# A graph layer with a softmax over sorted edges: its scans one after the other in place of side by side, and a first batch of 24 groups

## The chip, the cores and the metric

The kernel runs on one core of a Trainium2 chip. A core has five engines that run their own instruction streams and wait for one another through semaphores: TensorE (PE in the profile), VectorE (DVE), ScalarE (ACT), GpSimd (POOL) and SyncE (SP). Here SyncE and ScalarE also start plain transfers, and GpSimd starts the indirect ones, the gathers. The metric is the device time of one execution in microseconds (us).

## The reference

The program is one attention layer of a graph network and a layer norm. There are 12,500 nodes with 64 features, and 400,000 edges with 64 features, sorted by destination; all is float32.

```python
h_src, h_dst = x[src], x[dst]
e = leaky_relu(concat([h_src, h_dst, efeats]) @ W_attn + b_attn, 0.01)[:, 0]
m = concat([h_src, efeats]) @ W_ne
emax = segment_max(e, dst, N)
ex = exp(e - emax[dst])
alpha = ex / segment_sum(ex, dst, N)[dst]
z = segment_sum(alpha[:, None] * m, dst, N)
out = relu(concat([x, z]) @ W_out)
return layernorm(x + out)
```

## The kernel before

**Groups, parts, batches.** 512 edges form a group: 128 partitions with 4 edges each. There are 782 groups. Four groups are a part, which has a tile of edge features (`ze`) and a tile of gathered source rows (`zx`). Up to 32 groups are a batch, the unit of the softmax. Before, `sizes` is one batch of 4, then 37 of 20, then one each of 20, 10 and 8: 41 batches. Both tiles have ten buffers (`ZB`), two batches of five parts.

**The start.** While the node features come in, VectorE computes for each node its share of the score as a source and as a destination (L429, L432). The source score goes as a 65th column into a copy of the features in memory (`table`); the destination scores (`sdflat`) are copied out as a row of 48 neighbours for each node (`shifted`). Seven gathers take from it, for each group, the 48 scores that its destinations can have (`wk`, L469), and ScalarE's queue writes them to `wins`. Gathers that are issued ahead of these seven cannot take rows of `table`; they take rows of x (`plain`), and such a batch computes its source scores itself in `scores` (L194, L196). Before, the first batch of one part is plain. Each gather brings one row to each of 128 partitions, so a part is 16 gathers (L167).

**A batch.** `scores` computes, part by part, the score of each edge: the product with the edge weights and its sum (L190, L192), the source score (L197), a one-hot matrix of the edge's destination among 48 slots (L199), which picks the destination's score (L204, L207), and the leaky relu (L209). `softmax` then works on the whole batch. The scores are transposed (L295) so that a row holds 128 edges in order, and a segment's maximum and sum are formed by scans along rows. As a segment can cross rows, each scan is done in three steps: every row by itself, then one scan on a single partition over the ends of the rows, then every row again from its right start. `to_rows` brings the ends of the rows to one partition (a transpose L215 and four copies L218), `to_cols` brings the starts back (four copies L224 and a transpose L227). Before, forward and backward scans go through this together, as two blocks of one tile, once for the maximum and once for the sum. The sums give `alpha` (L347), and `fac`, by which the column that the batch shares with the one before is scaled (L374). `aggregate` weights the one-hot matrices with alpha (L358) and multiplies them with `ze` and `zx` on TensorE (L366); VectorE adds the result into `acc` at the group's first destination (L376). Masks for the next batch are prepared in the same stretch (L256 to L276). Finished blocks of nodes are written back in between (L498 to L529, "write-back" in what follows).

**Order.** A scheduler puts the instructions of each engine in order; VectorE then executes them in that order. A gather into a tile waits for the last matmul of the batch that had it, by a dependency written out in `gather`, so that all tiles of a batch come free together. GpSimd's queue holds the gathers in order and nothing else of note. The indices for the gathers come through TensorE transposes and a cast on VectorE (`srcs`, L134), in three buffers, so that a cast also waits for the gathers that still read the buffer.

Of the kernel before, what the change touches and what calls it, by code (L numbers as in the profile page):

```python
# [9 lines left out]
F32 = mybir.dt.float32  # L10
I32 = mybir.dt.int32
AF = mybir.ActivationFunctionType
OP = mybir.AluOpType
AX = mybir.AxisListType

P = 128
# [7 lines left out]
FLOOR = -1e31  # L24

S = 48
BG = 32
SG = 4
BS = 20
HQ = 4  # L30
# [10 lines left out]
def sorted_path(ctx, tc, x, dst, idx, edge, w_ne, w_attn, b_attn, w_out, out, flag):  # L41
# [6 lines left out]
    nc = tc.nc  # L48
# [11 lines left out]
    const = ctx.enter_context(tc.tile_pool(name="const", bufs=1))  # L60
# [5 lines left out]
    ones_row = const.tile([1, P], F32, name="ones_row")  # L66
    nc.vector.memset(ones_row, 1.0)

    turn = const.tile([P, 3, BG], F32, name="turn")
    nc.vector.memset(turn, 0.0)  # L70
    turn4 = const.tile([P, 4, BG], F32, name="turn4")
    nc.vector.memset(turn4, 0.0)
    b_col = const.tile([P, 1], F32, name="b_col")
    wne = const.tile([P, D], F32, name="wne")
    wout = const.tile([D, 2, D], F32, name="wout")
# [21 lines left out]
    tiny = loop.enter_context(tc.tile_pool(name="tiny", bufs=2))  # L97
# [111 lines left out]
        nc.vector.scalar_tensor_tensor(yb, sdst[:, 0:n], SLOPE, sdst[:, 0:n], op0=OP.mult, op1=OP.max)  # L209
        return hot  # L210

    def to_rows(pair):

        tr = rows.tile([P, 2, BG], F32, name="tr")
        nc.vector.transpose(tr, pair[:, :, 0:BG])  # L215
        row = tiny.tile([1, 2, P], F32, name="row", bufs=1)
        for h in range(HQ):
            nc.vector.tensor_copy(row.rearrange("o k (g h) -> o h k g", h=HQ)[:, h], tr[h * BG:h * BG + 1])  # L218
        return row

    def to_cols(row, n):

        for h in range(HQ):
            nc.vector.tensor_copy(turn[h * BG:h * BG + 1, 0:n, :],  # L224
                                  row[:, 0:n, 0:P].rearrange("o k (g h) -> o h k g", h=HQ)[:, h])
        ct = rows.tile([P, 3, BG], F32, name="ct", bufs=2)
        nc.vector.transpose(ct[:, 0:n, :].rearrange("r k g -> r (k g)"), turn[:, 0:n, :].rearrange("r k g -> r (k g)"))  # L227
        return ct

    def neighbours(g0, G):  # L230

# [19 lines left out]
    def softmax(G, y, d3, carry, first):  # L251


        R = HQ * G
        far = rows.tile([P, P + 2], F32, name="far3")
        nc.vector.tensor_scalar(far, d3, FAR, None, op0=OP.mult)  # L256

        pf = rows.tile([P, P], F32, name="pf")
        nc.vector.tensor_tensor(pf, far[:, 0:P], far[:, 1:P + 1], op=OP.subtract)
        pb = rows.tile([P, P], F32, name="pb")  # L260
        nc.vector.tensor_tensor(pb, far[:, 1:P + 1], far[:, 2:P + 2], op=OP.subtract)
        same = rows.tile([P, P], F32, name="same")
# [1 line left out]
        up = tiny.tile([P, 1], F32, name="up")  # L264
        nc.vector.tensor_reduce(up, pf, axis=AX.X, op=OP.max)
        nc.vector.tensor_tensor(worst[:, 1:2], worst[:, 1:2], up, op=OP.max)
        same_b = rows.tile([P, P], F32, name="same_b")
        nc.vector.tensor_scalar(same_b, pb, 0.0, None, op0=OP.is_ge)

        nc.vector.tensor_tensor(turn4[:, 0:2, 0], far[:, 0:2], far[:, P:P + 2], op=OP.subtract)  # L270
        nc.vector.tensor_scalar(turn4[:, 2:4, 0], turn4[:, 0:2, 0], 0.0, None, op0=OP.is_ge)
        tr4 = rows.tile([P, 4, BG], F32, name="tr4")
        nc.vector.transpose(tr4.rearrange("r k g -> r (k g)"), turn4.rearrange("r k g -> r (k g)"))
        rw = tiny.tile([1, 4, P], F32, name="rw", bufs=1)
        for h in range(HQ):
            nc.vector.tensor_copy(rw.rearrange("o k (g h) -> o h k g", h=HQ)[:, h], tr4[h * BG:h * BG + 1])  # L276

        mrow = tiny.tile([1, 2, P + 2], F32, name="mrow")
        srow = tiny.tile([1, 3, P + 2], F32, name="srow")
        ROW1 = P + 1  # L280
        flat_m = mrow.rearrange("o k i -> o (k i)")
        flat_s = srow.rearrange("o k i -> o (k i)")
        top, rtm = flat_m[:, 0:P + 1], flat_m[:, ROW1:ROW1 + P + 1]
        den, rts = flat_s[:, 0:P + 1], flat_s[:, ROW1:ROW1 + P + 1]
        nc.vector.memset(rtm[:, R:P + 1], FLOOR)
        nc.vector.memset(rts[:, R:P + 1], 0.0)
        if first:
            nc.vector.memset(top[:, 0:1], FLOOR)
            nc.vector.memset(den[:, 0:1], 0.0)
            nc.vector.memset(srow[:, 2, 0:P], 1.0)  # L290
        else:
            nc.vector.tensor_copy(top[:, 0:1], carry[0])

        er = rows.tile([P, T, P // T], F32, name="er")
        nc.vector.transpose(er.rearrange("r t q -> r (t q)"), y.rearrange("p t g -> p (t g)"))  # L295
        e = rows.tile([P, P], F32, name="e")
        nc.scalar.activation(e.rearrange("r (q t) -> r q t", t=T), er.rearrange("r t q -> r q t"), AF.Copy)
        pair = rows.tile([P, 2, P], F32, name="pair")
        nc.vector.tensor_tensor_scan(pair[:, 0, ::-1], pf, e, FLOOR, OP.add, OP.max)
        nc.vector.tensor_tensor_scan(pair[:, 1, ::-1], pb[:, ::-1], e[:, ::-1], FLOOR, OP.add, OP.max)  # L300
        row = to_rows(pair)
        nc.vector.tensor_tensor_scan(top[:, 1:P + 1], rw[:, 0, :], row[:, 0, :], top[:, 0:1], OP.add, OP.max)
        nc.vector.tensor_tensor_scan(rtm[:, 0:R][:, ::-1], rw[:, 1, 0:R][:, ::-1], row[:, 1, 0:R][:, ::-1],
                                     FLOOR, OP.add, OP.max)
        ini = to_cols(mrow, 2)
        s2 = rows.tile([P, P], F32, name="s2")
        nc.vector.tensor_tensor_scan(s2, pf, e, ini[:, 0, 0:1], OP.add, OP.max)
        b2 = rows.tile([P, P], F32, name="b2")
        nc.vector.tensor_tensor_scan(b2[:, ::-1], pb[:, ::-1], e[:, ::-1], ini[:, 1, 0:1], OP.add, OP.max)
        dl = rows.tile([P, P], F32, name="dl")  # L310
        nc.vector.tensor_tensor(dl, s2, b2, op=OP.max)
        nc.vector.tensor_tensor(dl, e, dl, op=OP.subtract)
        ex = rows.tile([P, P], F32, name="ex")
        nc.scalar.activation(ex, dl, AF.Exp)
        if not first:

            drop = tiny.tile([1, 2], F32, name="drop")
            nc.vector.tensor_tensor(drop[:, 0:1], top[:, 0:1], rtm[:, 0:1], op=OP.max)
            nc.vector.tensor_tensor(drop[:, 1:2], top[:, 0:1], drop[:, 0:1], op=OP.subtract)
            nc.scalar.activation(drop[:, 1:2], drop[:, 1:2], AF.Exp)  # L320
            nc.vector.tensor_tensor(den[:, 0:1], carry[1], drop[:, 1:2], op=OP.mult)
        pair = rows.tile([P, 2, P], F32, name="pair")
        nc.vector.tensor_tensor_scan(pair[:, 0, ::-1], same, ex, 0.0, OP.mult, OP.add)
        nc.vector.tensor_tensor_scan(pair[:, 1, ::-1], same_b[:, ::-1], ex[:, ::-1], 0.0, OP.mult, OP.add)
        row = to_rows(pair)
        nc.vector.tensor_tensor_scan(rts[:, 0:R][:, ::-1], rw[:, 3, 0:R][:, ::-1], row[:, 1, 0:R][:, ::-1],
                                     0.0, OP.mult, OP.add)
        nc.vector.tensor_tensor_scan(den[:, 1:P + 1], rw[:, 2, :], row[:, 0, :], den[:, 0:1], OP.mult, OP.add)
        if not first:

            fac1 = tiny.tile([1, 2], F32, name="fac1")
            nc.vector.tensor_tensor(fac1[:, 0:1], rts[:, 0:1], den[:, 0:1], op=OP.add)
            nc.vector.reciprocal(fac1[:, 1:2], fac1[:, 0:1])
            nc.vector.tensor_scalar(srow[:, 2, 0:P], den[:, 0:1].to_broadcast([1, P]), fac1[:, 1:2], None, op0=OP.mult)
        ini = to_cols(srow, 3)
        nc.vector.tensor_tensor_scan(s2, same, ex, ini[:, 0, 0:1], OP.mult, OP.add)
        sm = rows.tile([P, P], F32, name="b2")
        nc.vector.tensor_tensor_scan(sm[:, ::-1], same_b[:, ::-1], ex[:, ::-1], ini[:, 1, 0:1], OP.mult, OP.add)

        nc.vector.tensor_tensor(s2, s2, ex, op=OP.subtract)  # L340
        nc.vector.tensor_tensor(sm, sm, s2, op=OP.add)
        nc.vector.reciprocal(sm, sm)
        al = rows.tile([P, T, P // T], F32, name="al")
        nc.vector.tensor_tensor(al.rearrange("r t q -> r q t"), ex.rearrange("r (q t) -> r q t", t=T),
# [3 lines left out]
        nc.scalar.activation(alpha, alpha0, AF.Copy)  # L348
        fac = None
        if not first:  # L350
            fac = tiny.tile([P, 1], F32, name="fac")
            nc.vector.tensor_copy(fac, ini[:, 2, 0:1])
        return fac, (top[:, R:R + 1], den[:, R:R + 1])

    def aggregate(g0, n, ze, zx, hot, b0, fac):
# [24 lines left out]
    sizes = []  # L380
# [4 lines left out]
    while left > 0:  # L385
        sizes.insert(0, min(left, BS))
        left -= sizes[0]
    starts = [sum(sizes[:k]) for k in range(len(sizes))]


# [22 lines left out]
    ahead = [gather(0, min(SG, sizes[0]), prepared[0][0], 0, True)]  # L413
# [6 lines left out]
    with before:  # L420

        before.enter_context(tc.issue_after(casts[0]))
        for c0 in range(0, NB, CB):
            c1 = min(c0 + CB, NB)
            n = c1 - c0
# [10 lines left out]
            if c0 == 3 * CB:  # L436
                d0f = pre.tile([1, NG], F32, name="d0f", bufs=1)
                nc.vector.tensor_copy(d0f, d0i)
                for g0 in range(0, NG, 3 * P):
                    n = min(3 * P, NG - g0)  # L440
                    pb = psum.tile([P, SG, P], F32, name="pg", bufs=4).rearrange("p k n -> p (k n)")
# [8 lines left out]
        zero = pre.tile([1, S], F32, name="zero", bufs=1)  # L450
        nc.vector.memset(zero, 0.0)
        nc.scalar.dma_start(out=sdflat[NB * P:NB * P + S].unsqueeze(0), in_=zero)
        while len(ahead) < 5 and (len(ahead) + 1) * SG <= sizes[0]:
            ahead.append(gather(len(ahead) * SG, SG, prepared[0][0], 0, True))
        NW = (NG + P - 1) // P
        d0p = pre.tile([P, NW], I32, name="d0p", bufs=1)
# [9 lines left out]
        for k in range(NW):  # L466
            m = min(P, NG - k * P)
# [6 lines left out]
    rows = loop.enter_context(tc.tile_pool(name="rows", bufs=1))  # L474
# [62 lines left out]
    k = 0  # L537
# [12 lines left out]
    with loop:  # L550
        carry = added = None
        done = []
        ready = {0: prepare(0), 1: prepare(1, listed(starts[1], sizes[1]))}
        for k, G in enumerate(sizes):
# [9 lines left out]
            for g0 in range(b0, b0 + G, SG):  # L564
                n = min(SG, b0 + G - g0)
# [4 lines left out]
            fac, carry = softmax(G, y, d3, carry, k == 0)  # L570
# [464 lines left out]
```

## Time and profile before

| | |
|---|---|
| time, median of 3 runs (lowest to highest) | 5173.82 us (5171.24 to 5175.08) |
| the profiled execution | 5171.24 us, span 5169.4 us |
| busy: POOL, DVE, PE, ACT | 2967.6 (57%), 2102.8 (41%), 654.6 (13%), 245.5 (5%) us |
| gathers (L167) from `table` and from x | 3112 and 16 |
| one gather, median interval between starts | 0.95 us, 1.25 us |
| moved by transfers | 249.24 MB, mean 48 GB/s |
| chain of work that ended last | issue 52%, DVE 26%, unknown queue 11%, PE 7% |

The profile comes from one execution. A row of a group gives the line of the kernel, the engine and the operation, the tiles that it writes and reads, how often it ran, the time that the engine was busy with it, the mean length of one in ns, and how long the engine had been idle just before, with what ended most of that. "issue" is time in which the engine waited for nothing that the profile shows, and "remote" a release by something that the profile does not know. In a timeline the first two numbers are the start, in us from the start of the span, and the length; the bracket has the idle time ahead of it. No engine is busy for much more than half of the span.

### The profile page before, as it was taken

The page shows a single profiled execution, that of the slowest core. Times are in us where ns is not written, and L with a number is a line of the kernel's source. Part 1 is how long each engine was busy: PE and PEld are TensorE (multiplying, and loading weights), DVE is VectorE, ACT ScalarE, POOL GpSimd, SP SyncE. Part 2 cuts the span into 40 slices and gives each one's busy share as a digit, 9 for nine tenths or more (in the row PEclk, how much of TensorE's full clock was granted, in tenths as well). Part 3 has the DMA queues.
Part 4 walks back from the last instruction along what each step waited for, and adds up shares of the span by engine and source line. Part 5 has one row for each costly group of instructions (what it writes and reads, how often), then busy time and mean ns, then how long its engine had stood idle before and what let it go on. Part 6 is the DMA issues. An engine that isn't in the chain of part 4 may idle for free.

```text
span 5169.4 us, 39994 instructions
## 1 busy us (share of the span) xinstructions
PE 654.6 (13%) x13346; PEld 608.8 (12%) x13346; DVE 2102.8 (41%) x5756; ACT 245.5 (5%) x527; POOL 2967.6 (57%) x3142
## 2 busy tenths in 40 slices
PE   0010000001111110111110110111111111111113
PEld 0010000001101010111110110110111111111113
DVE  4153343333343343443444344444344444444446
ACT  0000000000000000000000000000000000000001
POOL 4745665665556556556565655555555555555550
PEclk9985555555555555555555555555555555555555
DMA  7122222222222222222222222222222222222220
GB/s 134 28 50 47 47 47 47 47 47 46 49 46 47 46 49 47 49 47 49 47 49 47 49 48 47 48 48 47 49 48 48 48 48 48 48 47 47 47 44 11
DMA packets 304916, 249.24 MB, mean 48 GB/s; under 512 B 125446, under 2 KB 253870, under 8 KB 304699
## 3 DMA queue, kind: packets, MB, share of 16 engines
q0 software_dynamic: 100320, 104.46, 13.5%
q1 hardware_dynamic: 177690, 135.46, 9.6%
q10 hardware_dynamic: 26688, 6.67, 0.7%
q8 instruction: 107, 1.75, 0.1%
q14 instruction: 111, 0.90, 0.1%
HBM read 239.69 MB, written 9.07 MB: 48 GB/s over the span
## 4 chain that ended last, share of the span: by engine, by line
issue 52%; DVE 26%; another core or an unknown queue 11%; PE 7%; DMA 2%; SPq 1%; DVEq 1%; POOL 0%; ACT 0%; ACTq 0%
PE pg L366 5%; DVE prod L190 3%; DVE hot L199 2%; DVE y L192 2%; DVE acc L376 2%; DVE prod L204 1%; DVE sdst L207 1%; PE pg L513 1%; DVE turn L224 1%; DVE row L218 1%; DVE rw L276 1%; PE pg L512 1%; DVE tr L215 1%; DMA zx<-table,srcs 1%
## 5 line engine op out<-in xcount | busy, mean ns | idle before, releaser
L167 POOL DMA_INDIRECT zx<-table,srcs x3112 | 2942.0, 945 | 2007.7 <-PE pg L366 1018.8
L366 PE MATMUL pg<-w,ze 128*64 128x48 f32 x6256 | 470.2, 248 | 3531.4 <-DVE w L358 2031.3
L366 PEld LDWEIGHTS pg<-w,ze 128*64 128x64 f32 x6256 | 462.4, 165 | 3536.7 <-DVE w L358 1940.2
L366 PE MATMUL pg<-w,zx 128*64 128x48 f32 x6256 | 471.3, 248 | 30.4 <-issue 30.3
L366 PEld LDWEIGHTS pg<-w,zx 128*64 128x64 f32 x6256 | 462.0, 165 | 32.6 <-issue 32.6
L218 DVE COPY row<-tr 1x64 f32<-1x64 f32 x328 | 77.0, 235 | 554.4 <-issue 459.6
L192 DVE TENSOR_REDUCE y<-prod 128x16 f32<-128x1024 f32 x196 | 237.6, 1212 | 4.8 <-remote 4.8
L190 DVE TENSOR_TENSOR prod<-ze,fixed 128x1024 f32<-128x1024 f32 x196 | 237.3, 1211 | 0.0
L376 DVE TENSOR_TENSOR acc<-acc,pg 128x48 f32 x782 | 154.3, 197 | 140.5 <-remote 85.5
L207 DVE TENSOR_REDUCE sdst<-prod 128x16 f32<-128x768 f32 x196 | 186.1, 949 | 27.1 <-issue 11.2
L204 DVE TENSOR_TENSOR prod<-hot,win 128x768 f32<-128x768 bf16 x196 | 186.4, 951 | 2.5 <-DVE y L197 2.0
L199 DVE TENSOR_TENSOR hot<-fixed,drel 128x768 bf16<-128x768 f32 x196 | 185.8, 948 | 0.0
L358 DVE TENSOR_TENSOR w<-hot,fixed 128x768 f32<-128x768 bf16 x196 | 175.9, 947 | 18.9 <-ACT fixed L348 18.8
L134 DVE CAST srcs<-pp 128x80 int32<-128x80 f32 (+3 forms) x41 | 9.4, 230 | 336.1 <-DMA zx<-table,srcs 333.3
L224 DVE COPY turn<-mrow 1x64 f32<-1x64 f32 x164 | 37.0, 226 | 266.7 <-issue 245.4
L131 PE MATMUL pp<-ident,nat 20*128 20x20 f32 (+3 forms) x328 | 42.7, 270 | 737.4 <-issue 402.1
L131 PEld LDWEIGHTS pp<-ident,nat 20*128 20x128 f32 (+3 forms) x328 | 39.2, 198 | 745.2 <-issue 722.5
L186 ACT ACTIVATE win<-wrow 128x192 f32<-128x192 f32 x196 | 64.9, 331 | 1147.8 <-DVE prod L204 768.1
L276 DVE COPY rw<-tr 1x128 f32<-1x128 f32 x164 | 45.8, 279 | 178.5 <-issue 160.7
L215 DVE STREAM_TRANSPOSE tr<-pair 128x64 f32<-128x64 f32 x82 | 20.1, 245 | 213.1 <-remote 189.9
L348 ACT ACTIVATE fixed<-alpha 128x128 f32<-128x128 f32 x41 | 11.5, 281 | 1929.6 <-DVE alpha L347 1895.2
L224 DVE COPY turn<-srow 1x96 f32<-1x96 f32 x164 | 50.9, 310 | 124.4 <-issue 122.3
(131 smaller groups left out, 1228.6 us busy)
## 6 DMA issues: line engine op xcount, KB each, us to landing
ze<-in_edge_dram SPq DMA_DIRECT2D x194, 512.0 KB
zx<-table,srcs POOLq DMA_INDIRECT x3112
wrow<-wins SPq DMA_DIRECT2D x195, 96.0 KB
table<-xt ACTq DMA_DIRECT2D x14, 227.5 KB
xb<-in_x_dram ACTq DMA_DIRECT2D x24, 128.0 KB
out_dram<-yo SPq DMA_DIRECT2D x24, 128.0 KB
raw<-in_idx_dram SPq DMA_DIRECT2D x38, 80.0 KB
xt<-in_x_dram SPq DMA_DIRECT2D x13, 224.0 KB
```

The costliest lines, as they stand in the source:

```text
L167: got = nc.gpsimd.indirect_dma_start(out=zx[:, g, t, 0:D] if plain else zx[:, g, t, :], out_offset=None, in_=x[:, :] if plain else table[: ...
L190: nc.vector.tensor_tensor(prod[:, 0:n], ze[:, 0:n], w_edge.unsqueeze(1).to_broadcast([P, n, T, D]), op=OP.mult)
L192: nc.vector.tensor_reduce(yb, prod[:, 0:n], axis=AX.X, op=OP.add)
L199: nc.vector.tensor_tensor(hot[:, 0:n], slots.unsqueeze(1).unsqueeze(1).to_broadcast([P, n, T, S]), drel[:, :, b:b + n].rearrange("p t g -> ...
L204: nc.vector.tensor_tensor(at[:, 0:n], hot[:, 0:n], win[:, 0:n].unsqueeze(2).to_broadcast([P, n, T, S]), op=OP.mult)
L207: nc.vector.tensor_reduce(sdst[:, 0:n], at[:, 0:n], axis=AX.X, op=OP.add)
L218: nc.vector.tensor_copy(row.rearrange("o k (g h) -> o h k g", h=HQ)[:, h], tr[h * BG:h * BG + 1])
L224: nc.vector.tensor_copy(turn[h * BG:h * BG + 1, 0:n, :], row[:, 0:n, 0:P].rearrange("o k (g h) -> o h k g", h=HQ)[:, h])
L276: nc.vector.tensor_copy(rw.rearrange("o k (g h) -> o h k g", h=HQ)[:, h], tr4[h * BG:h * BG + 1])
L358: nc.vector.tensor_tensor(w[:, 0:n], hot[:, 0:n], alpha[:, :, b:b + n].rearrange("p t g -> p g t").unsqueeze(3).to_broadcast([P, n, T, S]) ...
L366: last = nc.tensor.matmul(pg[at:at + D, g, :], z[:, g, t, 0:D], w[:, g, t, :], start=(t == 0), stop=(t == T - 1))
L376: added = nc.vector.tensor_tensor(ag, ag, pg[:, g, :], op=OP.add)
```

## The change

The change has two parts.

`softmax` no longer runs its two directions side by side. The forward scan of the maximum is completed first (a scan, `to_row`, a scan on one partition, `to_col`, a scan); the backward scans then run over its result, so that they give the maximum of the whole segment. The sum goes the same way. So there are four round trips of a row of 32 values per partition group where there were two of a pair of rows. The mask of the backward direction for the sum (`same_b`) goes, as do the maximum of the two directions and the subtraction and addition that joined the two sums. `fac` is no longer carried through `to_cols`, but is brought to all partitions by four copies and a transpose of its own. In the program after, these lines are: `to_row` L215 and L218, `to_col` L228 and L223, the row scans L283, L293, L298, L306, L314 and L327, the scans on one partition L290, L302 and L325, alpha L334, fac L339 to L344, the weights L350, the matmuls L358, the scaling and the additions L366 and L368.

The first two batches are joined into one of 24 groups, six parts, which leaves 40 batches. All six parts are gathered from x, ahead of the seven gathers of the destination scores.

```diff
-    def to_rows(pair):
-        tr = rows.tile([P, 2, BG], F32, name="tr")
-        nc.vector.transpose(tr, pair[:, :, 0:BG])
...
+    def to_row(block):
+        tr = rows.tile([P, BG], F32, name="tr")
+        nc.vector.transpose(tr, block)
+        row = tiny.tile([1, P], F32, name="row", bufs=1)
+        for h in range(HQ):
+            nc.vector.tensor_copy(row.rearrange("o (g h) -> o h g", h=HQ)[:, h, :], tr[h * BG:h * BG + 1, :])
...
+    def turned():
+        ct = rows.tile([P, BG], F32, name="ct", bufs=2)
+        nc.vector.transpose(ct, turn)
...
+    def to_col(row):
+        for h in range(HQ):
+            nc.vector.tensor_copy(turn[h * BG:h * BG + 1, :], row.rearrange("o (g h) -> o h g", h=HQ)[:, h, :])
+        return turned()
...
-        nc.vector.tensor_scalar(same_b, pb, 0.0, None, op0=OP.is_ge)
...
-        nc.vector.tensor_tensor_scan(pair[:, 0, ::-1], pf, e, FLOOR, OP.add, OP.max)
-        nc.vector.tensor_tensor_scan(pair[:, 1, ::-1], pb[:, ::-1], e[:, ::-1], FLOOR, OP.add, OP.max)
-        row = to_rows(pair)
...
-        ini = to_cols(mrow, 2)
...
+        nc.vector.tensor_tensor_scan(s1[:, ::-1], pf, e, FLOOR, OP.add, OP.max)
+        ends = to_row(s1[:, 0:BG])
...
+        nc.vector.tensor_tensor_scan(top[:, 1:P + 1], rw[:, 0, :], ends, top[:, 0:1], OP.add, OP.max)
+        ini = to_col(top[:, 0:P])
+        nc.vector.tensor_tensor_scan(s2, pf, e, ini, OP.add, OP.max)
+        def total(s, name):
+            nc.vector.tensor_tensor_scan(b1[:, ::-1], pb[:, ::-1], s[:, ::-1], FLOOR, OP.add, OP.max)
+            begins = to_row(b1[:, 0:BG])
...
+            nc.vector.tensor_tensor_scan(rt[:, 0:R][:, ::-1], rw[:, 1, 0:R][:, ::-1],
+                                         begins[:, 0:R][:, ::-1], FLOOR, OP.add, OP.max)
+            bi = to_col(rt[:, 1:P + 1])
+            nc.vector.tensor_tensor_scan(b2[:, ::-1], pb[:, ::-1], s[:, ::-1], bi, OP.add, OP.max)
+            return rt, b2
+        rtm, mx = total(s2, "m")
+        nc.vector.tensor_tensor(dl, e, mx, op=OP.subtract)
...
+        rts, sm = total(s2, "s")
...
+            nc.vector.reciprocal(fac1, rts[:, 0:1])
+            nc.vector.tensor_tensor(fac1, fac1, den[:, 0:1], op=OP.mult)
+            for h in range(HQ):
+                nc.vector.tensor_copy(turn[h * BG:h * BG + 1, :], fac1.to_broadcast([1, BG]))
...
+            nc.vector.tensor_copy(fac, turned())
...
+    if sizes[0] + sizes[1] <= BG:
+        sizes[0:2] = [sizes[0] + sizes[1]]
...
-        while len(ahead) < 5 and (len(ahead) + 1) * SG <= sizes[0]:
+        while len(ahead) < 6 and (len(ahead) + 1) * SG <= sizes[0]:
             ahead.append(gather(len(ahead) * SG, SG, prepared[0][0], 0, True))
```

## The prediction

> **What bounds the kernel now.** I read the page's groups first, then the timelines of GpSimd and VectorE through a batch in mid kernel, then the same code where no gather runs. The profiled execution took 5171.24 us (span 5169.4 and 1.8 around it), 2.6 below the median of 5173.82. Sums are made on 5171.2 and moved up by 2.6 at the end.
>
> The groups (busy us, mean ns, idle us before and its releaser) say that GpSimd's gathers are busy 57% of the span and idle otherwise, mostly until matmuls free the tiles, and that the smallest copies on VectorE have the longest idle times.
>
> ```profile
> L167 POOL DMA_INDIRECT zx<-table,srcs x3112 | 2942.0, 945 | 2007.7 <-PE pg L366 1018.8
> L218 DVE COPY row<-tr 1x64 f32<-1x64 f32 x328 | 77.0, 235 | 554.4 <-issue 459.6
> L224 DVE COPY turn<-mrow 1x64 f32<-1x64 f32 x164 | 37.0, 226 | 266.7 <-issue 245.4
> ```
>
> The timeline of GpSimd (start, length): a burst of 80 gathers, 1.25 us apart, lasts 99.8 us in every batch; this one began at 2632.2.
>
> ```profile
> 2731.04 0.94 POOL L167 DMA_INDIRECT zx<-table,srcs  x1 [0.30 <-issue]
> 2760.58 0.94 POOL L167 DMA_INDIRECT zx<-table,srcs  x1 [28.60 <-PE pg L503]
> ```
>
> Within that burst VectorE runs softmax's four row copies 1.4 to 2.1 us apart; after the last burst of the kernel the same four take 0.89 us in all.
>
> ```profile
> 2672.32 0.21 DVE L218 COPY row<-tr 1x64 f32<-1x64 f32 x1 [1.15 <-DVE tr L215]
> 2674.40 0.21 DVE L218 COPY row<-tr 1x64 f32<-1x64 f32 x1 [1.87 <-issue]
> 2675.80 0.21 DVE L218 COPY row<-tr 1x64 f32<-1x64 f32 x1 [1.19 <-issue]
> 2677.21 0.22 DVE L218 COPY row<-tr 1x64 f32<-1x64 f32 x1 [1.20 <-issue]
> ...
> 5086.24 0.24 DVE L215 STREAM_TRANSPOSE tr<-pair 128x64 f32<-128x64 f32 x1
> 5086.52 0.89 DVE L218 COPY row<-tr 1x64 f32<-1x64 f32 x4
> ```
>
> From L295 to the end of L347 softmax takes mostly 80 to 93 us beside a burst and 16.0 without (5084.7 to 5100.7). TensorE is slowed as well where its matmuls fall into a burst: one in 2.8 us.
>
> ```profile
> 262.08 0.24 PE L366 MATMUL pg<-w,ze 128*64 128x48 f32 x1 [2.56 <-issue]
> 264.88 0.24 PE L366 MATMUL pg<-w,ze 128*64 128x48 f32 x1 [2.56 <-issue]
> ```
>
> And where VectorE stood 33 us at L134's cast until the gathers landed, some 16 instructions came at full pace and the next were slow again:
>
> ```profile
> 577.39 0.24 DVE L134 CAST srcs<-pp 128x80 int32<-128x80 f32 x1 [32.93 <-DMA zx<-table,srcs]
> 577.55 0.88 DVE L218 COPY row<-tr 1x64 f32<-1x64 f32 x4
> ...
> 580.13 0.95 DVE L224 COPY turn<-srow 1x96 f32<-1x96 f32 x3
> 581.96 0.31 DVE L224 COPY turn<-srow 1x96 f32<-1x96 f32 x1 [0.88 <-issue]
> 583.36 0.27 DVE L276 COPY rw<-tr 1x128 f32<-1x128 f32 x1 [1.09 <-issue]
> ```
>
> I read this as instructions arriving slowly while gathers run, from a store that a long wait refills; that is inferred. The burst ended at 575.7, so slow spacing outlives it by 8 to 10 us. Hence a cycle: alpha, 13.6 us of weights and matmuls (alpha 2492.2, gather 2505.8), 99.8 us of burst, 8.5 us of slow spacing, then what is left of softmax at full pace. Batches with a write-back repeat at 129.6 us: 14.3 from the burst's end to alpha, 15.5 from alpha to the next burst.
>
> **Side-by-side softmax taken out.** In a middle batch before, the chain has 20 one-partition copies (8 L218, 8 L224, 4 L276); after, 40 (16, 16, 4, and 4 for fac). Four round trips follow one another, where two carried both directions. Removed are same_b, the maximum, and the two operations that join the sums. In the instruction order of both programs VectorE has 163 instructions from a batch's last w to the next alpha transpose before and 172 after (+9), and 12 more behind that transpose and ahead of the last w: six stand before the first w, six beside TensorE's first matmuls (1.2 us of VectorE waiting before, L376), at nothing; uncovered they cost 1.0. The six before w cost 1.1 us less the 0.66 that the copy of alpha took anyway: 0.45.
>
> The rest follows from where the chain stands when slow spacing ends. In a write-back batch L295 comes 33 us after the burst's start, which leaves 99.8 + 8.5 - 33 = 75 us. Before, 20 copies took 1.91 us each in it and 38 others 0.97 each (means over twenty batches), and what was left runs in 3 to 4 us at the quiet pace. After, by the same means, the third return to columns is reached with 24 copies (46 us) and 23 others (22 us), 68 in all; 7 us more bring the scans L327 and L298, L215 and a first copy. Left: 3 copies, scan, 4 copies, transpose, scan L306, fac's copies, 0.9 us of reciprocal, product and transpose: 6.8 us by the quiet rows. So +2.9 to +3.8, with w 3.3 to 4.2; I take 3.6. Ends: 9 instructions at 0.2 and 0.4 for w give 2.2; the whole surplus of slow time, 20 x 1.91 - 11 x 0.97 = 27.5 us, shrunk by 16/80 to the quiet pace, with w and 1 us uncovered, gives 7. A gain is excluded, since the instructions on that stretch become more. 31 batches: 112 us (68 to 217).
>
> In five early batches L134 again holds VectorE until the burst has landed, with 45 rows of the program behind it where before there were 30: quiet 13.2 us against 8.2, with w 5.5 each, 28 us (20 to 45). The last three softmaxes lie mostly beyond gathers: 14 to 17 instructions more, 4 us each, 12 (8 to 18). Together +152 (96 to 280).
>
> Two rules of the Trainium skill bear on the slow copies. "SBUF — State Buffer", Who interferes with whom, has copies lock a port pair against GpSimd for one instruction at a time and says that TensorE never waits. By it, as an estimate, 20 copies more would wait one gather of 0.94 us each, 19 us a batch, and the sum would be near 5790; the 2.8 us matmuls, and the slow rows behind the burst's end, disagree with it. "Runtime: NRT & Kernel Launch", Instruction fetch mechanics, has fetching hidden behind dispatch. By it, as an estimate, a softmax of 16 or 20 us would be over long before the burst is, and only the saving at the start would be left, 5106; the copies 1.4 us apart, which wait for nothing that the profile shows, contradict it.
>
> **First batch of 24.** Before, four groups were done alone: alpha at 199.4, but its matmuls, begun at 205.4, crept inside the 151 gathers that ran to 271.4, and L376 waited 85.5 us for them (to 294.5). Group 24 had its alpha at 336.2, group 44 at 463.2. After: 96 gathers from x start at 5.5; the first 16 took 22.8 us, 80 more at 1.25 make 128, with 4 for the preparation beside them 132. The seven gathers of the destination scores go behind all of them in GpSimd's queue, to 141 instead of 91; behind them wait wins, wrow and the first L204. Four parts of batch 1 (64 gathers) run to 221; the fifth waits for batch 0's tiles. Scores resume at 145 (before: 4 us after the seventh), six parts of 8.3 us plus stalls, 58: softmax from 203. Slow spacing ends at 230; about 50 instructions are left, 12 us: alpha at 242. Matmuls then meet no burst. With 15.5 us for six parts, 96 gathers (120 us) and 14.6 behind the burst as before, batch 1's alpha is at 242 + 15.5 + 120 + 15 = 393 to 397 against 463.2: 68 us saved. Ends: shifted was ready at 82.6; with SP, ACT and VectorE slowed by gathers from 28 us on I put it at 110 to 120, hidden ahead of 132. If it is 38 us late, 30 are saved; if the scores run at full pace, 85.
>
> The sum: 5171.2 + 152 - 68 = 5255; with 2.6, **5258 us**. Ends: 5171.2 + 96 - 85 = 5182 and 5171.2 + 280 - 30 = 5421.
>
> **Rivals.** *The longer chain fits under the burst* (faster): what is bought back after the burst is under 1.8 us a batch, the point at which 38 batches no longer outweigh 68; at nothing it gives 5106. For it: some batches have alpha 8 us after a burst (batch 17). Against: 14.3 in most, with the same work left. 11%, most of it near 5150. *The early gathers starve the preparation*: the destination scores come late, only 20 saved or none, 5306 to 5330. For it the 2.8 us matmuls; against it the 12 us in hand. 9%. *The slow spacing follows VectorE, not the burst*: then 27.5 us a batch, 36 times, near 6100; against it, spacing recovers 8 to 12 us after every burst. 3%. *The change does less than it says*: it does not; the order has 96 gathers ahead of the seven and 40 batches for 41.
>
> **How the numbers follow.** My forecast, the sum within its ends, has 77%. About 0.2%, 10 us, is what can be told from no change. From all cases: faster 0.11, same 0.06, slower 0.83. The range of 5185 to 5350 leaves out the faster rival, the 6100 and the forecast's top.
>
> **What would show it.** After: alpha 16 to 21 us behind a burst where it was 14.3, write-back batches repeating at 132 to 134 us with bursts still 99.8; copies in a burst still 1.4 apart; groups 24 and 44 with alpha near 242 and 395; no 85 us wait of L368 on matmuls. I am wrong if bursts lengthen, if tails stay at 14, or if the seven gathers are held past 140.

## The result, and the profile after

The changed kernel took 5239.23 us (median of 4 runs, 5236.72 to 5243.24) against 5173.3 for before beside it: ratio 1.0128, 95% interval 1.0111 to 1.0146, slower by 66 us. The profiled execution of after has a span of 5241.5 us, 72.1 more than before's 5169.4; the sums below are made on these spans.

One thing has to be known to read the numbers that follow. The kernels ran in five sets, each on one chip, and **before itself** took (as a median) 5173 us in the first set (the prediction's), 5159 in the second, 4338 in the third, 5173 in the fourth and 4331 in the fifth. The second and fourth set ran on one chip, the third and fifth on two others; the first set's chip is not on record. Ratios are always within a set. What sets these times apart is the pace of VectorE's instructions inside a burst of gathers; I call it *spaced* (sets one, two, four) and *full* (three, five). The prediction was made from a spaced profile and tested at that pace.

After's page has these groups (busy us, mean ns, idle us ahead and who ended most of it):

```profile
L167 POOL DMA_INDIRECT zx<-table,srcs x3032 | 2866.0, 945 | 2099.9 <-PE pg L358 1156.0
L218 DVE COPY row<-tr 1x32 f32<-1x32 f32 x640 | 133.1, 208 | 860.8 <-issue 681.3
L368 DVE TENSOR_TENSOR acc<-acc,pg 128x48 f32 x782 | 154.1, 197 | 33.6 <-PE pg L358 29.6
```

A gather is no longer or shorter (945 ns). The row copies, 640 for 328, have 861 us of idle time ahead of them where they had 554: 1.35 us each, 1.69 before, when each carried twice as much. The accumulation's idle time fell from 140.5 to 33.6 us, and the one wait of 85 us in the first batch, which the profile marks remote, is gone. Before had this line:

```profile
L376 DVE TENSOR_TENSOR acc<-acc,pg 128x48 f32 x782 | 154.3, 197 | 140.5 <-remote 85.5
```

The waits of GpSimd (us in total, times, longest), of before and then of after, show where the time is:

```profile
POOL zx L167 <- PE pg L366: 1018.8, 36, 34.8
...
POOL wk L469 <- DMA shifted<-sdflat: 54.4, 1, 54.4
```

```profile
POOL zx L167 <- PE pg L358: 1156.0, 36, 52.0
```

Both kernels run 3135 gathers. On average before waits 28 us between two bursts and after 32 (one of after's, behind the first burst, is 52), and after has no wait for `shifted`.

The timeline of one middle batch, GpSimd's rows and then VectorE's, mirrors the one shown of before:

```profile
4052.99 0.94 POOL L167 DMA_INDIRECT zx<-table,srcs  x1 [0.30 <-issue]
4085.84 0.95 POOL L167 DMA_INDIRECT zx<-table,srcs  x1 [31.91 <-PE pg L358]
```

```profile
3992.97 0.18 DVE L218 COPY row<-tr 1x32 f32<-1x32 f32 x1 [1.20 <-DVE tr L215]
3995.03 0.18 DVE L218 COPY row<-tr 1x32 f32<-1x32 f32 x1 [1.88 <-issue]
3996.43 0.18 DVE L218 COPY row<-tr 1x32 f32<-1x32 f32 x1 [1.21 <-issue]
...
4069.41 0.30 DVE L334 STREAM_TRANSPOSE alpha<-al 128x128 f32<-128x128 f32 x1
```

The copies are still 1.4 us apart, alpha comes 15.8 us behind the burst's end (4053.9) and the next burst 32 behind it, where before had 14.3 and 28.6. The start, GpSimd's rows around the destination scores and VectorE's first transposes of scores and of alpha:

```profile
130.54 0.94 POOL L167 DMA_INDIRECT zx<-in_x_dram,srcs  x1 [0.31 <-issue]
131.78 0.94 POOL L463 DMA_INDIRECT wk<-shifted,d0p  x1 [0.30 <-issue]
...
219.18 0.95 POOL L167 DMA_INDIRECT zx<-table,srcs  x1 [0.30 <-issue]
272.17 0.94 POOL L167 DMA_INDIRECT zx<-table,srcs  x1 [52.04 <-PE pg L358]
```

```profile
219.54 0.31 DVE L279 STREAM_TRANSPOSE er<-y 128x128 f32<-128x128 f32 x1 [1.21 <-DVE y L209]
255.87 0.31 DVE L334 STREAM_TRANSPOSE alpha<-al 128x128 f32<-128x128 f32 x1
296.24 0.31 DVE L279 STREAM_TRANSPOSE er<-y 128x128 f32<-128x128 f32 x1
406.00 0.30 DVE L334 STREAM_TRANSPOSE alpha<-al 128x128 f32<-128x128 f32 x1
```

A point in the program is named here, as in the prediction, by the number of groups done: at group 24 alpha comes at 256 (before 336), at group 44 at 406 (before 463).

### The profile page after: what moved, and what is told of

It reads as the page before. It is cut to its first block, busy times and chain, and to the rows that moved or that the text cites. A ratio compares the mean times of both kernels' runs of the same rounds, so it can differ in the third digit from the quotient of the medians.

```text
span 5241.5 us, 40850 instructions
## 1 busy us (share of the span) xinstructions
PE 652.8 (12%) x13338; PEld 611.2 (12%) x13338; DVE 2206.0 (42%) x6530; ACT 243.5 (5%) x522; POOL 2969.8 (57%) x3142
## 4 chain that ended last, share of the span: by engine, by line
issue 58%; DVE 27%; PE 7%; another core or an unknown queue 5%; DMA 1%; POOL 1%; DVEq 1%; SPq 0%; ACT 0%; ACTq 0%; POOLq 0%
PE pg L358 5%; DVE prod L190 2%; DVE hot L199 2%; DVE acc L368 2%; DVE row L218 2%; DVE sdst L207 2%; DVE turn L228 1%; DVE tr L215 1%; DVE y L192 1%; DVE prod L204 1%; POOL zx L167 1%; DMA zx<-table,srcs 1%; PE pg L507 1%; PE pg L506 1%
## 5 line engine op out<-in xcount | busy, mean ns | idle before, releaser
L167 POOL DMA_INDIRECT zx<-table,srcs x3032 | 2866.0, 945 | 2099.9 <-PE pg L358 1156.0
L358 PE MATMUL pg<-w,ze 128*64 128x48 f32 x6256 | 478.7, 250 | 3637.3 <-DVE w L350 2156.8
L358 PEld LDWEIGHTS pg<-w,ze 128*64 128x64 f32 x6256 | 471.5, 168 | 3644.5 <-DVE w L350 2047.1
L218 DVE COPY row<-tr 1x32 f32<-1x32 f32 x640 | 133.1, 208 | 860.8 <-issue 681.3
L358 PE MATMUL pg<-w,zx 128*64 128x48 f32 x6256 | 479.5, 251 | 0.0
L358 PEld LDWEIGHTS pg<-w,zx 128*64 128x64 f32 x6256 | 471.2, 168 | 0.0
L350 DVE TENSOR_TENSOR w<-hot,fixed 128x768 f32<-128x768 bf16 x196 | 175.8, 947 | 1.9 <-PE pg L358 0.7
L368 DVE TENSOR_TENSOR acc<-acc,pg 128x48 f32 x782 | 154.1, 197 | 33.6 <-PE pg L358 29.6
L228 DVE COPY turn<-rt_m 1x32 f32<-1x32 f32 x160 | 31.8, 199 | 233.4 <-issue 206.0
L167 POOL DMA_INDIRECT zx<-in_x_dram,srcs x96 | 96.4, 1004 | 33.6 <-issue 28.8
L228 DVE COPY turn<-top 1x32 f32<-1x32 f32 x160 | 34.1, 213 | 161.1 <-issue 159.6
L134 DVE CAST srcs<-pp 128x80 int32<-128x80 f32 (+3 forms) x40 | 9.5, 237 | 217.2 <-DMA zx<-table,srcs 210.4
L228 DVE COPY turn<-den 1x32 f32<-1x32 f32 x160 | 32.7, 204 | 152.1 <-issue 150.6
```

The costliest lines, as they stand in the source:

```text
L167: got = nc.gpsimd.indirect_dma_start(out=zx[:, g, t, 0:D] if plain else zx[:, g, t, :], out_offset=None, in_=x[:, :] if plain else table[: ...
L218: nc.vector.tensor_copy(row.rearrange("o (g h) -> o h g", h=HQ)[:, h, :], tr[h * BG:h * BG + 1, :])
L228: nc.vector.tensor_copy(turn[h * BG:h * BG + 1, :], row.rearrange("o (g h) -> o h g", h=HQ)[:, h, :])
L350: nc.vector.tensor_tensor(w[:, 0:n], hot[:, 0:n], alpha[:, :, b:b + n].rearrange("p t g -> p g t").unsqueeze(3).to_broadcast([P, n, T, S]) ...
L358: last = nc.tensor.matmul(pg[at:at + D, g, :], z[:, g, t, 0:D], w[:, g, t, :], start=(t == 0), stop=(t == T - 1))
L368: added = nc.vector.tensor_tensor(ag, ag, pg[:, g, :], op=OP.add)
```

## The experiments

My theory was the prediction's: at the spaced pace every instruction added to softmax costs a small price at the end of its batch, and the larger first batch saves its time once, at the start. The rivals: the two halves do not add up; VectorE's slow instructions are held at the memory port that it shares with GpSimd; the longer softmax fits under the burst.

**The two halves apart (second set, spaced; before 5159.3).** The batch alone is before with

```diff
+    if sizes[0] + sizes[1] <= BG:
+        sizes[0:2] = [sizes[0] + sizes[1]]
...
-        while len(ahead) < 5 and (len(ahead) + 1) * SG <= sizes[0]:
+        while len(ahead) < 6 and (len(ahead) + 1) * SG <= sizes[0]:
```

> The side-by-side softmax of before stays; only the first batch becomes 24 groups, with all six of its parts gathered from x ahead of the destination scores. Theory (the two halves of the change add up, the start saves what it saved in the changed kernel): batch 0's scores end near 219 as there, its softmax is 5 to 8 us shorter, alpha of group 44 comes near 398 to 402 where before had 463.2, and the rest runs as in before: 61 to 65 us less, 5108 us (5100 to 5118). Rival one (the gain at the start is given back by later stages, which wait for something else): 5150 or more. Rival two (the longer tails of the changed kernel come from the new batches, not from the softmax): write-back batches repeat at 132 us here too and the time is near 5220.

Measured: 5086.6 us, ratio 0.9862 (0.9845 to 0.9878), 73 us less, somewhat more than expected. Group 44 has its alpha at 380.7, ahead of the end of its burst (387.4):

```profile
380.36 0.31 DVE L347 STREAM_TRANSPOSE alpha<-al 128x128 f32<-128x128 f32 x1 [2.29 <-issue]
```

Its matmuls then crept until the burst was over and the next alpha came 144 us later; group 64 stands at 525.1 where the first profile of before has 590.0, and that 65 is the start's saving. Write-back batches repeat mostly at 129.4 to 130.7 us, so the longer tails do not come from the new batches. Of what ran at the spaced pace this is the quickest, ahead of both before and after; at the full pace that is the changed kernel with rw on ScalarE, below.

The softmax alone is the changed kernel without the merge:

```diff
-    if sizes[0] + sizes[1] <= BG:
-        sizes[0:2] = [sizes[0] + sizes[1]]
```

> The softmax with its passes one after another, and the batches of before (4, then 20). Theory: write-back batches repeat at 131.5 to 133.5 us where before had 129.6 to 130.1, alpha comes 15.5 to 18 us behind each burst, which is +124 us over the middle of the kernel, +4 in the last batches, and +2 to +10 in the first two softmaxes: 5173 + 135 = 5308 us (5292 to 5322). Rival (the longer tails come from the new batches): 5180 to 5200. Rival (extra softmax work fits under the burst in all but a few batches): under 5240.

Measured: 5288.8 us, ratio 1.0250 (1.0233 to 1.0267), 129.5 us more, near the 135 expected. Write-back batches repeat at 131.4 to 133.0 us. The two halves add up to +57 us with about 12 on either side; the changed kernel's own figures are +66 and, in the fourth set, +74. At group 64 they agree better: -64.9 and +9.3 for the halves, -51.4 for both.

**Where the destination scores stand (same set).**

```diff
-        while len(ahead) < 6 and (len(ahead) + 1) * SG <= sizes[0]:
+        while len(ahead) < 1 and (len(ahead) + 1) * SG <= sizes[0]:
```

> The changed kernel with its batch of 24, but only the first of the six parts gathered from x ahead of the destination scores' seven gathers; the other five parts are gathered from the table behind them, as before did with its second batch. Theory (the order of the gathers is worth the time in which GpSimd waits for the destination scores): the seven gathers come near 83 to 91, the 144 others behind them run to about 271, softmax of batch 0 runs inside that burst and its alpha comes 8 to 17 us behind it, 280 to 290 where the changed kernel has 256; 25 to 35 us more, 5268 us (5255 to 5280). Rival (merging the batches alone does it, the order is worth nothing): 5239 within 6. Rival (80 gathers on the preparation's back cost more than they bring): under 5230.

Measured: ratio 1.0136 (1.0119 to 1.0153), the changed kernel's within the interval. The expectation was wrong in what the edit does: the other parts were still gathered from x, 75 gathers ahead of the seven and 21 behind them. The seven start at 106.9 rather than 131.8:

```profile
105.67 0.94 POOL L167 DMA_INDIRECT zx<-in_x_dram,srcs  x1 [0.30 <-issue]
106.92 0.94 POOL L463 DMA_INDIRECT wk<-shifted,d0p  x1 [0.30 <-issue]
...
115.65 0.94 POOL L167 DMA_INDIRECT zx<-in_x_dram,srcs  x1 [0.30 <-issue]
```

Yet softmax begins at 228.0 and alpha comes at 257.7, no earlier than 219.5 and 256.2. So the destination scores, 25 us sooner, bought nothing: batch 0's scores run through the first burst at the spaced pace and end with it (GpSimd's 167 gathers end at 221.5 here and at 220.1 in after). It also shows `shifted` ready by 107.

**Which instructions are slow (same set).** Before, with four kinds added ahead of the scan that makes s2:

```diff
+        for k in range(6):
+            nc.vector.tensor_copy(a0, a1)
+            nc.vector.tensor_copy(fixed[0:1, 448:480], fixed[0:1, 480:512])
+            nc.vector.memset(a2, 0.0)
+            nc.vector.tensor_tensor(a3, a1, a1, op=OP.add)
```

> Before, with 24 more VectorE instructions of 32 elements on one partition in each softmax, ahead of the scan that makes s2, in six rounds of four kinds: copy SBUF to SBUF, copy PSUM to PSUM, memset, addition of two SBUF operands. None is used. Theory (inside a burst instructions of every kind reach VectorE slowly): all four kinds start 1.1 to 1.5 us apart inside a burst and under 0.25 us apart in the last softmax, 24 x 1.3 = 31 us of slow time a batch, of which the work pushed past the burst costs its quiet price, 3 to 6 us a batch: 5173 + 170 = 5343 us (5290 to 5400). Rival (a copy waits for a gather at the port that VectorE shares with GpSimd): the PSUM copy and the memset come within 0.3 us of the instruction ahead of them, the two SBUF kinds 1 us or more behind; 12 us of slow time, 5210 to 5260. Rival (slow spacing follows VectorE's work and not the burst): 24 x 1.3 us in every batch in full, 5173 + 36 x 31 = 6290.

Measured: 5381.8 us, 222.5 more (ratio 1.0429, 1.0412 to 1.0447). The groups, with idle us ahead of all 246 of each kind, and four rows from inside a burst:

```profile
L310 DVE COPY fixed<-fixed 1x32 f32<-1x32 f32 x246 | 44.3, 180 | 136.0 <-remote 50.9 <-issue 46.8 <-DVE sdst L208 13.7
L309 DVE COPY pair<-pair 1x32 f32<-1x32 f32 x246 | 44.1, 179 | 173.9 <-remote 81.8 <-issue 50.0 <-DVE pair L312 39.6
...
L312 DVE TENSOR_TENSOR pair<-pair 1x32 f32<-1x32 f32 x246 | 41.8, 170 | 131.7 <-DVE pair L311 61.1 <-remote 39.0 <-issue 31.5
...
L311 DVE MEMSET pair<- 1x32 f32 x246 | 20.9, 85 | 243.0 <-remote 124.2 <-issue 79.7 <-DVE pair L309 32.9
```

```profile
2801.15 0.17 DVE L309 COPY pair<-pair 1x32 f32<-1x32 f32 x1 [1.85 <-remote]
2802.59 0.09 DVE L311 MEMSET pair<- 1x32 f32 x1 [1.26 <-DVE pair L309]
2803.95 0.18 DVE L312 TENSOR_TENSOR pair<-pair 1x32 f32<-1x32 f32 x1 [1.28 <-DVE pair L311]
2805.36 0.17 DVE L309 COPY pair<-pair 1x32 f32<-1x32 f32 x1 [1.23 <-DVE pair L312]
```

Copy, memset and addition follow one another at the same 1.4 us. The memset, which reads nothing, waits longest on average (0.99 us); the PSUM copies were mostly set among the scores by the instruction order, but the 65 of them that came more than 30 us into a burst waited 1.27 us each, by the timeline. That speaks against a port held by a gather. "SBUF — State Buffer" of the Trainium skill, Who interferes with whom, says that a VectorE instruction with at most one SBUF input does not contend with GpSimd outside the two-port modes; a memset and a copy within PSUM that wait as long as the rest are no contention by that page; what holds them would have another cause, which no run shows. The price: 24 instructions cost 684.6 us of idle time and 151.1 of busy time in 41 batches, 20 us a batch, but the kernel became 222.5 us longer; over the 38 batches with a burst that is 5.9 a batch, **0.24 us for an instruction**. Softmax's own instructions take about that at the quiet pace (62 rows in 16.0 us in before's last but one, 0.26 each), as they should if what the 24 push behind the burst pays the quiet price. It is not what the 24 themselves cost there: the last two softmaxes, where no gather runs, became 1.0 and 0.7 us longer; several of the 24 start 0.1 to 0.2 us apart there.

**Instructions taken off VectorE (third set, full pace; before 4337.9).** Softmax's one-partition copies were given to ScalarE, the four of rw alone or all of them:

```diff
-            nc.vector.tensor_copy(rw.rearrange("o k (g h) -> o h k g", h=HQ)[:, h], tr3[h * BG:h * BG + 1])
+            nc.scalar.activation(rw.rearrange("o k (g h) -> o h k g", h=HQ)[:, h], tr3[h * BG:h * BG + 1], AF.Copy)
```

> The changed kernel with softmax's four rw copies (L276) on ScalarE, which is idle for most of a burst; the other 36 one-partition copies stay on VectorE. Theory (a burst delivers instructions to VectorE slowly, and each one taken out of that stream pulls work forward out of the tail): 4 x 1.4 to 1.9 us of slow time, which at the price measured by the 24 added instructions (222 us over 40 batches, 0.23 us for one) is 0.9 us a batch, 37 us: 1.006 times before, 5190 us (5175 to 5205). Rival (rw's copies lie where the burst hides them): the changed kernel's ratio of 1.013, 5226 within 8. Rival (only an instruction that reads or writes the memory VectorE shares with GpSimd counts, and these four count in full): 5 us a batch or more, under 5060.

> The changed kernel with all 40 one-partition copies of softmax (rw, row, turn and fac) on ScalarE. Theory: VectorE's stream has 132 instructions for 172, ScalarE has few of its own and its copies start at about 0.25 us one behind another inside a burst; five round trips pay two hand-offs each, some 10 us in all; softmax needs 65 us of the burst where it needed 82, alpha comes at the burst's end or before, and what then sets the next burst is the weights and matmuls, which stay slow until some 10 us behind the burst: bursts follow one another at 25 us where the changed kernel has 31.5, 6 us a batch, 220 us less: 5005 us (4960 to 5080). Rival (ScalarE's instructions come as slowly as VectorE's): each copy still takes 1.2 us or more and the hand-offs come on top, 5220 or slower.

> Before's side-by-side softmax with the batch of 24 (5086.6 us in the run of that alone), and all 20 one-partition copies of softmax on ScalarE. Theory: 20 fewer in VectorE's stream, at 0.23 us for one 4.6 us a batch, but bursts cannot follow one another at less than about 25 us where they now have 25 to 30: 3 us a batch, 110 us: 4975 us (4940 to 5030). Rival (ScalarE's instructions come as slowly): no gain or a loss, 5080 to 5150.

> The batch of 24 with before's softmax, and only the four rw copies on ScalarE. Theory: 0.9 us a batch, 5086.6 - 35 = 5052 us (5035 to 5070). Rival (they lie where the burst hides them): 5087 within 8.

Measured, in ratios: the changed kernel with rw on ScalarE 0.9539 (0.9523 to 0.9555), with all copies there 0.9945 (0.9929 to 0.9962); the batch alone with all copies there 0.9638 (0.9622 to 0.9654), with rw there 0.9647 (0.9631 to 0.9663). No theory had foreseen such numbers, because before itself took 4338 us, and none of the four runs tests what it was meant to: there was no spacing to relieve. What a copy moved to ScalarE is worth at the spaced pace stays open.

**The changed kernel and before once more (fourth set, spaced; before 5173.1).** Neither kernel was edited.

> The changed kernel as it is. In the last four runs before itself took 4338 us where it had taken 5159 and 5173, and VectorE's instructions came at full pace inside the bursts. Theory (the sign of the change follows from the pace at which VectorE's instructions come): where before takes about 5160, the ratio is 1.0128 again, 5226 us; where it takes about 4340, the longer softmax lies wholly under a burst, the gathers run without a pause from batch 6 on, and the changed kernel is faster, ratio 0.954 to 0.957 as in the run with rw on ScalarE, 4140 to 4155 us. Rival (the gain of that run came from moving rw, and the change costs 1.3% whatever the pace): 1.01 times before in either case, 4390 us where before takes 4340.

> The kernel before as it is, for its trace beside the changed kernel's in the same set of runs. Theory: where it takes about 4340 us, VectorE waits at L134's cast until a burst has landed in more batches than the changed kernel does (five), about 12, and from then on the gathers run without a pause, at 100 us a batch where such a wait makes it 125. Rival: the batches repeat at an even pace of some 105 us. Where it takes about 5160: write-back batches repeat at 129.6 us as in the first profile.

Measured: ratio 1.0145 (1.0128 to 1.0162), 74 us more. Before's trace repeats the first: GpSimd waits 36 times for L366, 1025.4 us in all.

**The full pace once more (fifth set, before 4330.9).** The batch alone with all copies on ScalarE, and the changed kernel without any edit:

> The batch of 24 with before's softmax and its 20 one-partition copies on ScalarE once more, since its first set of runs (0.964 times before) had VectorE's instructions at full pace. Theory, where before takes about 5160 to 5173 and instructions come slowly inside bursts: 0.986 times before for the batch alone, and 20 instructions fewer on VectorE's stream at 0.23 us, held to 3 us a batch by the 25 us that a new burst needs behind the last one: 0.96 to 0.97 times before, 4965 to 5020 us. Rival (ScalarE's instructions come as slowly, and hand-offs come on top): 0.985 or more, 5095 us or slower. Where before takes about 4340: 0.964 again.

> The changed kernel once more, on whichever pace this set of runs has. Theory: where before takes about 5160 to 5173, 1.013 to 1.0145 times before. Where it takes about 4340, 0.954 to 0.957 (the longer softmax hidden under bursts that follow one another without a pause). Rival: slower than before by 1% at either pace.

Measured: the former 0.9655 (0.9639 to 0.9671); **the changed kernel 0.9606 (0.9590 to 0.9622), 172 us faster than before** (0.954 to 0.957 was expected at this pace). The same program that is 1.5% slower on the chip of the fourth set is 3.9% faster on that of the fifth. Its page and GpSimd's waits there:

```profile
L167 POOL DMA_INDIRECT zx<-table,srcs x3032 | 2869.9, 947 | 1085.4 <-issue 863.1
L134 DVE CAST srcs<-pp 128x80 int32<-128x80 f32 (+3 forms) x40 | 9.5, 238 | 972.7 <-DMA zx<-table,srcs 969.2
L218 DVE COPY row<-tr 1x32 f32<-1x32 f32 x640 | 145.0, 227 | 10.9
```

```profile
POOL zx L167 <- PE pg L358: 163.5, 7, 26.8
```

The same 640 row copies wait 10.9 us in all, for 860.8 in the first set. Gathers are as long (947 ns) and as far apart (1.25 us), and they run beside the copies:

```profile
2013.56 0.31 DVE L279 STREAM_TRANSPOSE er<-y 128x128 f32<-128x128 f32 x1
2015.53 0.88 DVE L218 COPY row<-tr 1x32 f32<-1x32 f32 x4
...
2033.72 0.30 DVE L334 STREAM_TRANSPOSE alpha<-al 128x128 f32<-128x128 f32 x1
```

```profile
2013.79 0.94 POOL L167 DMA_INDIRECT zx<-table,srcs  x1 [0.30 <-issue]
```

Softmax takes 20.5 us inside the gathers, where the first set's took 82. From 1002.8 to 4096.7 us GpSimd issues 2472 gathers without a pause, 100 us for the 80 of a batch: it has become the bound. What pauses are left come from another place (VectorE's casts, and the gather behind one of them):

```profile
851.60 0.24 DVE L134 CAST srcs<-pp 128x80 int32<-128x80 f32 x1 [71.02 <-DMA zx<-table,srcs]
978.04 0.24 DVE L134 CAST srcs<-pp 128x80 int32<-128x80 f32 x1 [71.72 <-DMA zx<-table,srcs]
1104.19 0.24 DVE L134 CAST srcs<-pp 128x80 int32<-128x80 f32 x1 [16.84 <-DMA zx<-table,srcs]
```

```profile
876.79 0.94 POOL L167 DMA_INDIRECT zx<-table,srcs  x1 [26.83 <-PE pg L358]
```

In batches 1 to 6 L134's cast stands inside softmax in VectorE's order, so VectorE waits there until the burst has landed, and the rest of softmax, the weights and the matmuls come behind it: a pause of GpSimd of about 26 us (22 for the first of the six). From batch 7 on the cast stands ahead of the scores' end and the chain is broken. Counted in VectorE's order in the traces, the cast stands inside softmax in 12 batches of before and in 6 of the changed kernel. In the runs at full pace it does so 5 times (the changed kernel with rw on ScalarE), 6 (the changed kernel), 7 (batch alone, rw on ScalarE) and 9 (batch alone, all copies there, in both sets), and GpSimd pauses by over 15 us just as often. The changed kernel with all copies on ScalarE has six such pauses too, but 13 more of 9.6 to 14.4 us.

At this pace the pauses are nearly all that sets these kernels apart. In the six executions profiled at it, GpSimd's waits for matmuls sum to between 151 and 325 us, and the span less these waits is 3982 to 3997 us in every one, while the spans themselves go from 4136 to 4314. Before was not profiled at that pace. If each of its 12 batches paused 24.5 us, the mean of the batch alone with rw on ScalarE, that would be 294 us against 154 in the changed kernel, 140 of the 172 us that the change gains there; this split is an estimate and not shown.

## Why the prediction was right, and where not

- **The cycle held.** Bursts of 99.8 us, copies 1.4 us apart, slow rows until 8 to 13 us behind the burst, L134's wait with some 16 instructions at full pace behind it: all as described.
- **Softmax, the term of 152 us: measured about 129.** The five early L134 batches cost 28.0 us more (28 was said). The next 30 batches cost 92.4 us more in sum, 3.1 each, where the prediction took 3.6; write-back batches repeat at 132.4 us on average (132 to 134 was said) for 129.8. Of the 3.1, the tail, from the burst's end to alpha, has 2.5 on average (15.7 for 13.2; 2.9 to 3.8 was worked out) and the stretch from alpha to the next burst 0.6 (0.45 was). Behind write-back batches the tails are mostly 15.8 us (15.3 to 16.6), just short of the 16 to 21 expected, and 18 in the early batches. In a late batch VectorE has 149 rows for 138 from the last weights to alpha and 16 for 6 from there to the last weights, +11 and +10, where the prediction counted +9 and +12. The last three batches cost 8.5 us with what follows the last alpha (3.2 for the last with gathers, 3.8 and 1.5), where 12 was taken.
- **The start, the term of 68 us: measured 57** (group 44 at 406.3 for 463.2, inside 30 to 85). The gathers went as said: seven ended at 140.2 (141) and the 64 at 220.1 (221). The step that failed is the scores of batch 0, 58 us from 145 in the working and 74.5 in the trace: three parts came at full pace behind a 51 us wait, the other three were spaced. Softmax began at 219.5, not 203, and took 36.6 us, not 39, so alpha was 14 late. The rest, 150.1 us to the next alpha, was given as 150.
- **The two errors nearly cancelled**: 129 - 57 = 72, the measured difference of the spans, against 152 - 68 = 84. L368 no longer has a wait of 85 us, as said. That before's wait was for matmuls is not shown: the 64 matmuls of the first batch had ended at 270.7, and VectorE and GpSimd went on together at 294.5 and 294.7, released by what the profile marks remote.
- **Luck had a part in it.** The prediction did not weigh that the pace could be another one. The result was measured at the pace of the profile that it was made from; in the fifth set the same forecast would have had the wrong sign.
- **The rivals.** *The early gathers starve the preparation*: `shifted` was ready by 107, the seven went out at 131.8 with no wait. *The slow spacing follows VectorE* at 27.5 us a batch: it was 3.1. *The longer chain fits under the burst*: false at the pace that the profile showed (batch 17, named for it with 8 us, has alpha 6.6 us behind its burst, but most batches have 14), true at the full pace, where the price a batch is nothing from batch 7 on. 5106 of 5171 would be 0.987, and 0.9606 was measured; the estimate above puts most of the rest on the batches in which L134's cast stands inside softmax, which the change halves. By the traces of the second set most of that comes from the new softmax, which alone leaves 7 of the 12; the merge alone leaves 9, both together 6. The prediction had those batches in its sums, but only as a place where more rows follow.
- **The reading behind it was too narrow.** "Instructions arrive slowly while gathers run" was inferred from a profile in which they do. The third and fifth set have the same gathers at the same spacing and no slow instructions. Gathers alone do not cause the spacing.

## What to carry to other kernels

Where instructions come at a fraction of their pace with no wait that the profile shows, price an edit by what is left when the pace recovers, not by what the instructions take inside: 24 instructions took 20 us of slow time and cost 5.9. Then ask whether the pace belongs to the program: here it does not, and the sign of the change turns with it. An instruction that waits for a whole burst (here a cast that overwrites indices) should not stand inside a chain that the next burst waits for; at the full pace its place in the engine's order made the pauses of 16 to 28 us.

## What the runs showed of the hardware

The pace inside a burst differs between the sets and, by the times, is the same for every run of a set: the row copies of one and the same program waited 1.35 us each in the first set and 0.02 in the fifth, and before's medians are 5159 to 5173 us or 4331 to 4338, nothing between. The chip is the likely cause: the one that ran two sets was spaced in both, with a set at full pace on another chip between them. But each of the two chips at full pace ran one set only, so that something else in a set decides is not ruled out. The granted clock is not it: before's runs show 0.574 to 0.578 in the second and fourth set and 0.564 to 0.577 in the third and fifth. Gathers (0.95 us, 1.25 apart) are alike in both, and so are the transfers of the queues marked instruction in the DMA section of the page, here of after in the first set and then in the fifth:

```profile
q8 instruction: 107, 1.75, 0.1%
q14 instruction: 116, 0.95, 0.1%
```

```profile
q8 instruction: 107, 1.75, 0.2%
q14 instruction: 116, 0.95, 0.1%
```

By these lines the blocks are fetched as often and about as briefly at either pace (on average 1.17 and 1.09 us on q8, 0.46 and 0.43 on q14), so the store that I inferred, which a long wait refills, would lie behind these transfers; no run showed it. "Runtime: NRT & Kernel Launch" of the Trainium skill, Instruction fetch mechanics, has fetching hidden behind dispatch: the 10.9 us of the fifth set agree with it, and the 860.8 of the first would not if that idle time is fetching, which is not shown. What makes a chip, or a set, spaced is open.
